# A convolution, attention and expert-mixture kernel on one core: the kv sum's constant part moved to PE, and three more slots for the last images' gate broadcasts

## The chip, the core and the metric

The kernel runs on one core of a Trainium2 chip. Its engines are TensorE (PE, matmuls; its weight loads are listed as PEld), VectorE (DVE), ScalarE (ACT), GpSimd (POOL) and SyncE (SP, which here only issues transfers); 16 DMA engines move data between the chip's memory (DRAM, HBM) and the core's on-chip memory. PE's results go to a memory of their own, PSUM, from which DVE and ACT read them. Each engine has its own program, built in a fixed order, in which an instruction waits until the semaphores that it names have come.

The metric is the time of one execution in microseconds of device time. Before the change five runs were made; the median counts. A profile is one more execution, recorded by the hardware.

## What is computed

The input `x` is 32 images of 128 channels by 56 by 56 pixels (3136 tokens of 128 numbers each, in float32). Cut to what matters here:

```python
x = x + conv3x3(sign(group_norm(x)), sign(w)) * Alpha       # layer 0
t = to_tokens(x)                                            # layer 1, by image: 3136 x 128
u = layer_norm(t)
q, k, v = u @ Wq + bq, u @ Wk + bk, u @ Wv + bv
kv = sum(k * v, axis=tokens)                                # one number for each channel
t = t + q * kv
u = layer_norm(t)
p = softmax(u @ router_w + router_b);  best two of 8 experts, their weights made to add to 1
t = t + sum of the two weights times (u @ expert_w[e] + expert_b[e])
```

The sum over tokens never needs k and v themselves. The layer norm's mean is taken out by centring the weights, so u is the tokens times the reciprocal deviation. With G = uᵀu (128 by 128, "gram"), s = the sum of u over the tokens (a column), n = 3136 and all vectors by output channel c,

`kv[c] = sum over d of Wk[d,c] * ((G Wv)[d,c] + bv[c]*s[d]) + bk[c] * (sᵀ Wv)[c] + n*bk[c]*bv[c]`

The change is about how this line is computed, and about the last step of the expert mixture.

## The kernel before

**Planner.** The kernel describes its work as some thousands of small steps with `at(due, key, engine, work, do, after, take, free, delay)`. `due` is when the step should come, `work` its length in microseconds as its author put it down, `after` the steps it needs, `take` and `free` the slots of a ring of buffers that it takes and frees. Before anything is emitted, `in_order` lays all steps out in time by these numbers, and the instructions are emitted in that order. So the order on each engine is fixed when the program is built. If a `work`, a ring or a dependency changes anywhere, the order of later steps can change on all engines.

**Images.** Images are worked on some 60 us apart by their due times, and two or three overlap: convolution of image i+1 (nine matmuls for each of seven stripes, `cv`), transposes to tokens (`xt`), statistics, `gram` of image i, the kv steps, projection `q` with the matrix `move`, routing on DVE, gates, experts. The x and token buffers are three each (`x_all`, `tok_all`, image i uses number i mod 3). Images 0 to 27 form four groups. Their first 8 or 12 token chunks take all eight experts ("dense"); the other tokens are sorted by pair of experts, sent to DRAM with indirect transfers, worked on in tiles (`turn`, `to`), and fetched back (`back`, then `back_ps`, copied to `o` and stored). Images 28 to 31 are in no group and all their 25 chunks are dense, so the kernel's end is dense work of images 30 and 31 with the fetching back of the last group laid between.

**The kv steps of one image.** They follow the gram matmuls and share one PSUM slot, ring `acc`, of size one. `gram_out` (L754, ACT) copies G and the column s to `g_sb`. `kv_1` (L758, PE) makes `gv` = G Wv. `kv_2` is three DVE operations: `prod` = bv*s + gv (L763), times Wk (L765), plus `wv_bk`*s (L767), where `wv_bk` = Wv*bk was made once. `kv_3` (L772, PE) sums `prod` over its 128 rows with a matmul by `ones`, which gives kv as a row repeated on all partitions. `kv_4` (DVE) adds the constant `n_bkbv` (L777), then makes the left part of `move` (L779) and `bq_kv` (L781). `kv_5` (L786, PE) turns kv into a column with a one-column matmul. `kv_6` (L792, L794, DVE) multiplies the router's weights by that column, and again by bq. `kv_7` (L801, L802, PE) makes two small products of it, `kv_8` (L806, L808, ACT) copies them into `move` and `cq`. Then `project` (L863) can start. `bias` (L815) adds `bq_kv` to the tokens on DVE.

**Set-up.** `prepare` runs once, after the first image's convolution: PE centres the weights (`centred`, L377 and L379), DVE makes `move`'s right part, `wv_bk` (L394), `n_bkbv` (L395), `masks` (L402) and, from the expert biases, `eb_sum` and `eb_w` (L407 to L415). All of DVE's set-up stands in DVE's order in the order in which the code issues it.

**Dense experts.** For a block b of four chunks (512 tokens) there are four units k = 0 to 3, each two experts. The gates of an image are transposed on PE (`gate_turn`, L1017), copied by ACT, and stored by SP to DRAM (`gate_store` L1038, `parts_store` L1061). `spread` (SP) loads from there: for k = 0 first `gt` (L1129, three transfers), then for every unit `bc` (L1132), the gates of two experts, 512 tokens each, repeated over 128 partitions, 512 KB. `bc` is a ring of four slots. `gated` (L1141, DVE) multiplies it with the tokens `tt`, which frees the slot; `experts` (L1153 and L1159, PE) does `eb_w` once in a block and two matmuls for each unit, 512 columns each; `finish` (L1170, DVE) and `store` (L1175, SP) end the block. SP issues everything in one order: loads of x, gates, broadcasts, result stores (L1175, and L1471 for the fetched-back blocks). A store that waits for its data holds everything behind it.

Of the kernel before, what the change touches and what calls it, by code (L numbers as in the profile page):

```python
# [54 lines left out]
C = 128  # L55
# [34 lines left out]

P = 60.0
# [8 lines left out]
    t_in=3, turned=2, v=3, w=2, back=12, sent=4, o=2,  # L100
# [85 lines left out]
def conv_attn_moe_kernel(  # L186
# [173 lines left out]
    wv_bk = const.tile([C, C], F32, name="wv_bk")  # L360
    n_bkbv = const.tile([C, C], F32, name="n_bkbv")
# [5 lines left out]
    def prepare():  # L367
# [25 lines left out]

        nc.vector.tensor_mul(wv_bk, wv_sb, bk_bc)  # L394
        nc.vector.scalar_tensor_tensor(  # L395
            n_bkbv, bk_bc, float(n_tok), bv_bc, ALU.mult, ALU.mult
        )

# [145 lines left out]
    def plan_image(i: int):  # L544
# [215 lines left out]
        def kv_2():  # L760
            tok_sum = d["g_sb"][:, C : C + 1]
            prod = spool.tile([C, C], F32, tag="prod", bufs=1, name=f"prod_{i}")
            nc.vector.scalar_tensor_tensor(prod, bv_bc, tok_sum, d["gv"], ALU.mult, ALU.add)  # L763
            yield
            nc.vector.tensor_mul(prod, prod, wk_sb)  # L765
            yield
            nc.vector.scalar_tensor_tensor(prod, wv_bk, tok_sum, prod, ALU.mult, ALU.add)  # L767
            d["prod"] = prod

        def kv_3():  # L770
            d["kv_ps"] = ps_acc.tile([C, C], F32, tag="acc", name=f"kv_ps_{i}")
            nc.tensor.matmul(d["kv_ps"], lhsT=ones, rhs=d["prod"], start=True, stop=True)  # L772

        def kv_4():

            kv = spool.tile([C, C], F32, tag="prod", bufs=1, name=f"kv_{i}")
            nc.vector.tensor_add(kv, n_bkbv, d["kv_ps"])  # L777
# [4 lines left out]
            d["kv"] = kv  # L782

        def kv_5():
            d["kvc"] = ps_acc.tile([C, 1], F32, tag="acc", name=f"kvc_ps_{i}")
            nc.tensor.matmul(d["kvc"], lhsT=d["kv"], rhs=ident[:, :1], start=True, stop=True)  # L786

        def kv_6():
# [3 lines left out]
            nc.vector.scalar_tensor_tensor(kr[:, 0, :], rw_sb, d["kvc"], one, ALU.mult, ALU.mult)  # L792
# [24 lines left out]
        for g in range(n_blk):  # L817
# [18 lines left out]
        for j, (engine, work, do) in enumerate(kv_steps, 1):  # L836
# [1041 lines left out]
```

## Time and profile before

| | us |
|---|---|
| median of 5 runs | 2284.51 |
| lowest and highest run | 2275.41, 2289.13 |
| profiled execution | 2265.75 |
| its span, first to last instruction | 2264.1 |
| PE idle in the span | 160 |
| PE idle from 100 to 500 | 33 |
| PE idle from 500 to 2040 | 78 |
| PE idle from 2100 to the end | 22 |

The profiled execution is 18.8 us shorter than the median of the timed runs, so a sum made from its rows belongs to 2265.75 and not to 2284.51. The granted TensorE clock was 0.975 of full on average. An engine's busy time doesn't hold the issuing of transfers, and the ends of matmuls are modelled; one float32 matmul shows as two records, each with its own weight load.

The memory traffic of the end is heavy: in the last fortieth of the span 291 GB/s were moved, against a mean of 198 over the whole.

### The profile page before, as it was taken

Reading aid. Unit: us, or ns where it says so; the run is one execution under the profiler, and the core shown is the slowest. Engines: PE = TensorE matmul, PEld = TensorE weight load, DVE = VectorE, ACT = ScalarE, POOL = GpSimd, SP = SyncE. Lnnn points to the kernel's source line nnn. Section 1 sums busy time; section 2 is a strip of 40 time slices with the busy share of each in tenths; the row PEclk is TensorE's granted clock in tenths of the full one; section 3 lists DMA queues with packets and bytes.
Section 4 is the critical chain, followed back from the end, with each engine's and each line's share of the span. In section 5 each row is a group of like instructions: output and inputs, shape, how many; then the busy total and the mean of one; then the engine's idle time right before and its main releaser. Section 6 shows DMA issues by size and latency. Waiting matters only on the chain.

```text
span 2264.1 us, 45320 instructions
## 1 busy us (share of the span) xinstructions
PE 2103.9 (93%) x12074; PEld 1449.0 (64%) x12074; DVE 1971.0 (87%) x6074; ACT 1527.6 (67%) x4917; POOL 1037.2 (46%) x1013
## 2 busy tenths in 40 slices
PE   5899999899999999989999999988999999999889
PEld 2666556556777776557776776655677666675544
DVE  4899999999999999878898889988888897789765
ACT  5667776667888887658777876655868776574311
POOL 3044443333333235656443544666654546234563
PEclk9999999999999999989999999999999999999899
DMA  4155544455655555567677766667768777878688
GB/s 167 30 168 167 171 155 151 139 176 188 193 163 152 184 175 170 170 203 252 175 218 232 228 194 202 215 202 244 231 177 250 210 211 244 257 217 267 209 278 291
DMA packets 324364, 448.58 MB, mean 198 GB/s; under 512 B 61832, under 2 KB 222128, under 8 KB 324112
## 3 DMA queue, kind: packets, MB, share of 16 engines
q1 hardware_dynamic: 294384, 382.80, 53.9%
q0 software_dynamic: 28144, 56.14, 8.1%
q10 hardware_dynamic: 1584, 6.75, 0.8%
q8 instruction: 102, 1.67, 0.3%
q14 instruction: 150, 1.23, 0.2%
HBM read 319.51 MB, written 126.00 MB: 197 GB/s over the span
## 4 chain that ended last, share of the span: by engine, by line
PE 42%; DVE 7%; issue 3%; ACT 3%; DMA 2%; SPq 1%; another core or an unknown queue 1%; POOL 0%; DVEq 0%; ACTq 0%; POOLq 0%
PE ff L1159 15%; PE cv L642 6%; PE to L1687 6%; PE gram L744 3%; PE q L863 3%; DVE gated L1141 2%; PE back_ps L1459 2%; PE xt L667 1%; PE turn L1669 1%; PE l L1114 1%; ACT v L1705 1%; DMA t_in<-rows 1%; DMA bc<-gp 1%; ACT w L1712 1%
## 5 line engine op out<-in xcount | busy, mean ns | idle before, releaser
L1365 POOL DMA_INDIRECT rows<-tok,row_no x428 | 510.6, 1193 | 580.7 <-ACT tok L1358 284.3
L1159 PE MATMUL ff<-gated,ew_d 128*128 128x512 f32 (+1 forms) x1536 | 708.6, 590 | 24.1 <-DVE gated L1141 15.6
L1444 POOL DMA_INDIRECT back<-res,res_no x428 | 495.3, 1157 | 446.0 <-PE back_ps L1459 249.3
L1141 DVE TENSOR_TENSOR gated<-tt,bc 128x1024 f32<-128x1024 f32 x384 | 449.9, 1178 | 75.0 <-PE ff L1159 31.4
L642 PE MATMUL cv<-xs,w_bin 128*128 128x440 bf16 (+3 forms) x2016 | 428.8, 361 | 19.0 <-ACT xs L599 10.9
L1159 PEld LDWEIGHTS ff<-gated,ew_d 128*128 128x128 f32 x1536 | 273.3, 192 | 259.6 <-issue 209.7
L1705 ACT ACTIVATE v<-to,t_in 128x128 f32<-128x128 f32 x528 | 255.1, 484 | 135.2 <-PE to L1687 68.2
L642 PEld LDWEIGHTS <-w_bin 128*128 128x128 bf16 x2016 | 199.2, 100 | 186.7 <-issue 37.8
L1687 PEld LDWEIGHTS to<-ew_s,turned 128*128 128x128 f32 x2112 | 261.2, 194 | 57.1 <-issue 30.2
L877 ACT ACTIVATE qs<-q,r 128x136 f32<-128x136 f32 (+1 forms) x800 | 248.3, 411 | 64.4 <-PE q L863 38.2
L1687 PE MATMUL to<-ew_s,turned 128*128 x2112 | 274.0, 279 | 16.9 <-ACT turned L1675 8.7
L735 ACT ACTIVATE y<-tok,r 128x128 f32<-128x128 f32 (+1 forms) x800 | 256.4, 426 | 26.2 <-remote 12.7
L863 PE MATMUL q<-move,x 128*128 128x144 f32 (+1 forms) x1600 | 242.8, 297 | 16.1 <-ACT move L806 5.6
L863 PEld LDWEIGHTS q<-move,x 128*128 128x128 f32 (+1 forms) x1600 | 215.7, 194 | 47.1 <-issue 19.2
L744 PEld LDWEIGHTS gram<-y 128*128 128x128 f32 (+1 forms) x1600 | 201.7, 192 | 47.5 <-issue 36.4
L744 PE MATMUL gram<-y 128*128 128x129 f32 (+1 forms) x1600 | 217.2, 280 | 6.3 <-issue 5.8
L682 DVE BATCH_NORM_STATS2 st<-tok 128x6 f32<-128x128 f32 (+1 forms) x800 | 184.8, 277 | 33.0 <-ACT tok L673 24.2
L1712 ACT ACTIVATE w<-to,t_in 128x128 f32<-128x128 f32 x528 | 208.8, 395 | 0.0
L893 DVE BATCH_NORM_STATS2 st<-tok 128x6 f32<-128x128 f32 (+1 forms) x800 | 198.0, 284 | 6.2
L673 ACT COPY tok<-xt 128x512 f32<-128x512 f32 (+1 forms) x224 | 121.6, 564 | 94.7 <-PE xt L667 65.9
L890 DVE TENSOR_TENSOR tok<-tok,qs 128x408 f32<-128x408 f32 (+1 forms) x288 | 155.8, 541 | 29.2 <-ACT tok L882 23.0
L653 DVE SCALAR_TENSOR_TENSOR x<-cv,alpha_col,x 128x448 f32<-128x448 f32 x224 | 150.8, 674 | 33.9 <-PE cv L642 10.2
(229 smaller groups left out, 2894.6 us busy)
## 6 DMA issues: line engine op xcount, KB each, us to landing
bc<-gp SPq DMA_DIRECT2D x368, 512.0 KB
x<-in_x_dram SPq DMA_DIRECT2D x116, 392.0 KB
t_in<-rows SPq DMA_DIRECT2D x528, 66.0 KB
res<-v SPq DMA_DIRECT2D x132, 256.0 KB
out_dram<-o SPq DMA_DIRECT2D x100, 256.0 KB
out_dram<-tt SPq DMA_DIRECT2D x92, 256.0 KB
rows<-zeros SPq DMA_DIRECT2D x116, 66.0 KB
rows<-tok,row_no POOLq DMA_INDIRECT x428
```

The lines of the kernel that those rows point to most:

```text
L642: nc.tensor.matmul(cv[:, r0:r1, c0:c1], lhsT=w_bin[:, t, :], rhs=xs[:, b * ROWS + dy + r0 : b * ROWS + dy + r1, dx + c0 : dx + c1], start= ...
L735: nc.scalar.mul(y[:n, j, :C], d["tok"][:n, c, :C], d["r1"][:n, c : c + 1])
L744: nc.tensor.matmul(d["gram"], lhsT=y[:n, j, :C], rhs=y[:n, j, :], start=(c == 0), stop=(c == n_ck - 1),)
L863: nc.tensor.matmul(p[:n, k, :], lhsT=d["x"][:, c * C : c * C + n], rhs=move, start=True, stop=True,)
L877: nc.scalar.mul(qs[:n, k, :], p[:n, k, : C + N_EXP], d["r1"][:n, c : c + 1])
L1141: nc.vector.tensor_tensor(g[:, :, :n], d["tt", b][:, :n].unsqueeze(1).to_broadcast([C, 2, n]), d.pop(("bc", b, k))[:, :, :n], ALU.mult,)
L1159: nc.tensor.matmul(d["ff", b][:, :n], lhsT=ew_d[:, e * C : (e + 1) * C], rhs=g[:, j, :n], start=False, stop=(e == N_EXP - 1),)
L1365: dma = nc.gpsimd.indirect_dma_start(out=groups[group]["rows"], out_offset=bass.IndirectOffsetOnAxis(ap=d["row_no"][:n, c - n_dense : c - ...
L1444: dma = nc.gpsimd.indirect_dma_start(out=d["back", c][:n, :], out_offset=None, in_=groups[group]["res"][: quads_of(group) * WIDE, :], in_o ...
L1687: nc.tensor.matmul(p[:, k, j, :], lhsT=t[:, n * C : (n + 1) * C], rhs=ew_s[:, bass.ds(d["cols", q][j][n], C)], start=True, stop=True,)
L1705: nc.scalar.activation(d["v", q][:, n, :], p[:, k, 0, :], AF.Identity, bias=row[:, C + 2 : C + 3], scale=row[:, C : C + 1],)
L1712: nc.scalar.mul(d["w", q][:, n, :], p[:, k, 1, :], row[:, C + 1 : C + 2])
```

## The change

It has two parts, and the second has no data in common with the first.

**The kv sum.** The term with bv is merged into the constant matrix: `wv_bk` becomes Wv*bk + Wk*bv, made in the set-up. `kv_2` is one DVE operation, `prod` = Wk * gv. `kv_3` makes four matmuls into one PSUM tile of 129 columns: s repeated as stationary operand (a read with step 0) times `wv_bk`, plus `ones` times `prod`, give the row on all partitions; `prod` times a column of `ones`, plus `wv_bk` times s, give the same sums as a column. `kv_5` is gone. `kv_6` reads the column from that tile and adds the constant `rw_n`, the router's weights times n*bk*bv as a column, for which the set-up has one more matmul (`n_col_ps`) and one more DVE operation. `kv_6` and `kv_4` both follow `kv_3`. In the planner `kv_3` counts 0.70 in place of 0.25, `kv_2` 0.21 in place of three pieces.

**Three more slots.** From image 30 on every second unit's broadcast (of seven units the 2nd, 4th and 6th) goes to a third of the x buffer of image 29, which nothing reads after that image's projection. This is a ring `late` of three beside `bc` of four. The transfer itself has the same size and the same queue.

```diff
+LATE, LATE_IN = 30, 29
...
+        wk_bv = spool.tile([C, C], F32, tag="prod", bufs=1, name="wk_bv")
+        nc.vector.tensor_mul(wk_bv, wk_sb, bv_bc)
         nc.vector.tensor_mul(wv_bk, wv_sb, bk_bc)
+        nc.vector.tensor_add(wv_bk, wv_bk, wk_bv)
         nc.vector.scalar_tensor_tensor(
             n_bkbv, bk_bc, float(n_tok), bv_bc, ALU.mult, ALU.mult
         )
+        p = ps.tile([C, 1], F32, tag="ps", name="n_col_ps")
+        nc.tensor.matmul(p, lhsT=n_bkbv, rhs=ident[:, :1], start=True, stop=True)
+        nc.vector.tensor_scalar(rw_n, rw_sb, p, None, ALU.mult)
...
+    n_late = n_tok // (2 * WIDE)
+
+    def late_of(i, n):
+
+        turn = n % (2 * n_late + 1)
+        return turn // 2 if i >= LATE and turn % 2 else None
...
         def kv_2():
-            tok_sum = d["g_sb"][:, C : C + 1]
-            prod = spool.tile([C, C], F32, tag="prod", bufs=1, name=f"prod_{i}")
-            nc.vector.scalar_tensor_tensor(prod, bv_bc, tok_sum, d["gv"], ALU.mult, ALU.add)
-            yield
-            nc.vector.tensor_mul(prod, prod, wk_sb)
-            yield
-            nc.vector.scalar_tensor_tensor(prod, wv_bk, tok_sum, prod, ALU.mult, ALU.add)
-            d["prod"] = prod
+            d["prod"] = spool.tile([C, C], F32, tag="prod", bufs=1, name=f"prod_{i}")
+            nc.vector.tensor_mul(d["prod"], wk_sb, d["gv"])
 
         def kv_3():
-            d["kv_ps"] = ps_acc.tile([C, C], F32, tag="acc", name=f"kv_ps_{i}")
-            nc.tensor.matmul(d["kv_ps"], lhsT=ones, rhs=d["prod"], start=True, stop=True)
+            p = ps_acc.tile([C, C + 1], F32, tag="acc", name=f"kv_ps_{i}")
+            tok_sum = d["g_sb"][:, C : C + 1]
+            nc.tensor.matmul(
+                p[:, :C], lhsT=tok_sum.to_broadcast([C, C]), rhs=wv_bk, start=True, stop=False
+            )
+            nc.tensor.matmul(p[:, :C], lhsT=ones, rhs=d["prod"], start=False, stop=True)
+            nc.tensor.matmul(p[:, C:], lhsT=d["prod"], rhs=ones[:, :1], start=True, stop=False)
+            nc.tensor.matmul(p[:, C:], lhsT=wv_bk, rhs=tok_sum, start=False, stop=True)
+            d["kv_ps"] = p
...
-        def kv_5():
-            d["kvc"] = ps_acc.tile([C, 1], F32, tag="acc", name=f"kvc_ps_{i}")
-            nc.tensor.matmul(d["kvc"], lhsT=d["kv"], rhs=ident[:, :1], start=True, stop=True)
...
-            nc.vector.scalar_tensor_tensor(kr[:, 0, :], rw_sb, d["kvc"], one, ALU.mult, ALU.mult)
+            nc.vector.scalar_tensor_tensor(
+                kr[:, 0, :], rw_sb, d["kv_ps"][:, C:], rw_n, ALU.mult, ALU.add
+            )
...
-            ("PE", 0.25, kv_1), ("DVE", [0.26, 0.21, 0.27], kv_2), ("PE", 0.25, kv_3), ("DVE", [0.19, 0.41], kv_4),
-            ("PE", 0.25, kv_5), ("DVE", [0.14, 0.14], kv_6), ("PE", 0.46, kv_7), ("ACT", 0.15, kv_8),
...
+            (1, "PE", 0.25, kv_1, ["gram_out"], ["acc"], []),
+            (2, "DVE", 0.21, kv_2, ["kv_1"], [], [("acc", ("kv_1", i))]),
+            (3, "PE", 0.70, kv_3, ["kv_2"], ["acc"], []),
+            (4, "DVE", [0.19, 0.41], kv_4, ["kv_3"], [], [("acc", ("kv_3", i))]),
+            (6, "DVE", [0.14, 0.14], kv_6, ["kv_3"], [], [("acc", ("kv_3", i))]),
+            (7, "PE", 0.46, kv_7, ["kv_6"], ["acc"], []),
+            (8, "ACT", 0.15, kv_8, ["kv_7", "kv_4"], [], [("acc", ("kv_7", i))]),
...
-            bc = bpool.tile([C, 2, WIDE], F32, tag="bc", bufs=4, name=f"bc_{i}_{b}_{k}")
+            slot = late_of(i, b * N_EXP // 2 + k)
+            if slot is None:
+                bc = bpool.tile([C, 2, WIDE], F32, tag="bc", bufs=4, name=f"bc_{i}_{b}_{k}")
+            else:
+                bc = x_all[LATE_IN % HELD][:, slot * 2 * WIDE : (slot + 1) * 2 * WIDE]
+                bc = bc.rearrange("c (j t) -> c j t", j=2)
...
+                bc_ring = "bc" if late_of(i, n) is None else "late"
...
+                    + (
+                        [("project", LATE_IN, j) for j in range(len(q_groups))]
+                        if bc_ring == "late"
+                        else []
+                    ),
+                    take=[bc_ring] if k else [bc_ring, "gt"], delay=SPREAD_LANDS,
```

More of the change, by code (lines that the diff above doesn't have):

```diff
@@ L832, in plan_image @@
         kv_steps = (
-            ("PE", 0.25, kv_1), ("DVE", [0.26, 0.21, 0.27], kv_2), ("PE", 0.25, kv_3), ("DVE", [0.19, 0.41], kv_4),
-            ("PE", 0.25, kv_5), ("DVE", [0.14, 0.14], kv_6), ("PE", 0.46, kv_7), ("ACT", 0.15, kv_8),
-        )
-        for j, (engine, work, do) in enumerate(kv_steps, 1):
-            after = [(f"kv_{j - 1}", i) if j > 1 else ("gram_out", i)]
+            (1, "PE", 0.25, kv_1, ["gram_out"], ["acc"], []),
[5 more added lines that the diff above has]
+            (8, "ACT", 0.15, kv_8, ["kv_7", "kv_4"], [], [("acc", ("kv_7", i))]),
+        )
+        for j, engine, work, do, after, take, free in kv_steps:
+            after = [(k, i) for k in after]
             if j == 4:
@@ L841, in plan_image @@
                 after += [("route_1", i - 2), ("project", i - 2, 8)]
-            at(
-                s + 75 + j, (f"kv_{j}", i), engine, work, do, after=after,
-                take=["acc"] if engine == "PE" else [],
-                free=[] if engine == "PE" else [("acc", (f"kv_{j - 1}", i))],
-            )
+            at(s + 75 + j, (f"kv_{j}", i), engine, work, do, after=after, take=take, free=free)
         for g in range(n_blk):
@@ L1206, in plan_image @@
                     + [("gated", i, n - 1) if n else ("gated", i - 1, last_unit)],
-                    take=["gated"], free=[("bc", ("spread", i, n))], slack=0.5,
+                    take=["gated"], free=[(bc_ring, ("spread", i, n))], slack=0.5,
                 )
```

11 lines of the change are left out of this document (5 added, 6 removed).

## The prediction

> **What bounds the kernel now.** I read the busy shares first, then busy time by stretch, then the groups of the kv steps, then the timeline at the three places where the change moves something: the set-up, the last image's kv chain, the last image's gates.
>
> ```profile
> PE 2103.9 (93%) x12074; PEld 1449.0 (64%) x12074; DVE 1971.0 (87%) x6074; ACT 1527.6 (67%) x4917; POOL 1037.2 (46%) x1013
> ```
>
> By the whole span PE is the bound, with DVE behind it. By stretch (columns: stretch, length, busy PE, PEld, DVE, ACT, POOL, granted clock, DMA share, GB/s) it is not one story:
>
> ```profile
> 100.00:500.00 400.00, 367.05 (x2063) 240.52 (x2061) 387.90 (x1371) 272.64 (x917) 168.95 (x160) 0.97 0.47 152
> 500.00:2040.00 1540.00, 1462.00 (x8810) 1045.88 (x8810) 1354.53 (x4127) 1133.86 (x3644) 739.31 (x628) 0.98 0.67 206
> 2100.00:2126.00 26.00, 19.15 (x102) 13.26 (x100) 18.61 (x48) 5.36 (x15) 13.88 (x13) 0.86 0.51 165
> 2136.00:2184.00 48.00, 44.31 (x143) 21.13 (x144) 43.23 (x95) 9.69 (x28) 32.29 (x27) 1.00 0.92 301
> 2184.00:2214.00 30.00, 21.88 (x68) 11.40 (x69) 12.61 (x22) 3.48 (x10) 19.25 (x19) 0.72 0.78 244
> 2214.00:2264.00 50.00, 46.86 (x152) 23.32 (x151) 29.54 (x32) 6.73 (x14) 15.20 (x13) 0.98 0.81 287
> ```
>
> From 100 to 500 DVE sets the pace (97%, while PE has 33 us free); from 500 to 2040 PE does (95%); at 2100 to 2126 and 2184 to 2214 neither does, and the clock drops: two stalls of the last image.
>
> The kv steps in the groups (busy us, mean ns of one | idle of the engine before them and what ended it; one f32 matmul is two records):
>
> ```profile
> L767 DVE SCALAR_TENSOR_TENSOR prod<-wv_bk,g_sb,prod 128x128 f32<-128x128 f32 x32 | 11.0, 344 | 1.0 <-DVE st L682 0.6
> L763 DVE SCALAR_TENSOR_TENSOR prod<-bv_bc,g_sb,gv 128x128 f32<-128x128 f32 x32 | 10.9, 342 | 10.6 <-PE gv L758 7.6 <-PE gt_ps L1017 2.8
> L772 PE MATMUL kv_ps<-prod,ones 128*128 128x128 f32 x64 | 13.9, 297 | 4.8 <-DVE prod L767 3.5 <-issue 1.3
> L786 PE MATMUL kvc_ps<-ident,kv 128*128 128x1 f32 x64 | 10.2, 229 | 7.0 <-issue 3.7 <-DVE kv L777 3.3
> ```
>
> **Part 1, set-up: +2.4.** Program order of the changed kernel: n_col_ps is PE's last set-up matmul, and DVE's rw_n, which reads it, stands ahead of masks, eb_sum, eb_w, a conv_add (L653) and the total of image 2 (L588).
>
> ```profile
> 43.17 0.28 DVE L395 SCALAR_TENSOR_TENSOR n_bkbv<-bk_bc,bv_bc 128x128 f32<-128x128 f32 x1
> 45.91 0.22 DVE L415 CAST eb_w<-eb_sum 72x128 bf16<-72x128 f32 x1
> 48.47 0.60 PE L667 MATMUL xt<-ident,x 128*128 128x128 f32 x4
> 49.22 0.16 DVE L596 TENSOR_SCALAR neg_gm<-gm_ps 128x1 f32<-128x1 f32 x1 [2.04 <-PE gm_ps L592]
> ```
>
> Now DVE goes straight on. Then it stands from 43.9 (0.56 later, for two more 128x128 operations) until PE's set-up ends at 48.5 plus 0.14 for n_col_ps, so about 49.1; behind it 2.7 us (43.4 to 46.1) to eb_w, 0.4 of statistics and 0.6 of conv_add, giving 52.8. PE's xt needs that conv_add: 52.9 instead of 48.5, and behind it the group mean, the signs, and image 1's convolution. +4.4. Some comes back at once: between gv and the first q of image 0 PE's order holds 6 us of other work instead of 12 (13.1 us went by, 67.90 to 81.02), so q of image 0 starts earlier; from 0 to -5, I take -2 because the displaced convolutions still have to run.
>
> **Part 2, DVE: -5.6 where DVE sets the pace.** Two of three prod operations go: 342 + 344 = 0.69 us, with their gaps 0.70. The column's kr stays one operation. Eight chains lie in 100 to 500: -5.6. The added matmuls there (8 x 0.36, next part) lie in PE's 33 us of idle time; without that cover they cost 2.9. Elsewhere DVE's gain (22 x 0.70 from 500 to 2040) is off the path, where DVE is 88% busy.
>
> **Part 3, PE: +4 where PE sets the pace.** kv_3 grows from one 128x128 matmul to two plus two of one column; kv_5's column matmul goes. Net one 128x128 and one 128x1. In a full queue a gram matmul takes 0.22 (eight records in 0.89), and kvc_ps 0.14 (2040.20 to the next start at 2040.34): +0.36 per image, 22 chains from 500 to 2040, +7.9. The lowest bound is 0 (all of it in idle time), the highest the unhidden records, 2 x 0.297 + 2 x 0.229 = 1.05 each, +23. I take the queue's pitch, as these matmuls stand in a full queue. No row has a stationary operand read with step 0, as tok_sum is now; its nearest is an ordinary load, 0.19, hidden under matmuls. Against it stand waits that ended at kv_ps, kvc_ps, kr_ps or the first q: 9.4 us from 500 to 2040 in PE's waits. The chain loses two DVE operations, one trip PE-DVE-PE and DVE work queued ahead of kr, but the planner also gives it less cover; I take -4 of 0 to -9.
>
> **Part 4, last kv chain: -4.** Nothing is left to cover it:
>
> ```profile
> 2117.35 0.49 PE L772 MATMUL kv_ps<-prod,ones 128*128 128x128 f32 x2 [0.32 <-issue]
> 2121.49 0.58 PE L786 MATMUL kvc_ps<-ident,kv 128*128 128x1 f32 x2 [3.66 <-issue]
> 2124.16 0.60 PE L801 MATMUL kr_ps<-kr,wq_t 128*128 128x8 f32 x2 [2.08 <-DVE kr L792]
> 2126.38 6.13 PE L863 MATMUL q<-move,x 128*128 128x144 f32 x24 [0.89 <-ACT move L806]
> ```
>
> From gv's end (2116.2) to q is 10.2 us, 3.6 of them DVE waits before finish and kv that no row explains (2.45, 1.19). The new chain: prod 0.29, four matmuls about 1.1, kv 0.29, kr 0.22, move 0.29, bq_kv 0.28, kr 0.22, kr_ps 1.1, move 0.17, some 0.4 for hops: 4.4. So -2.2 if the unexplained waits stay, -5.8 if they go. Then 24 q records took 6.13 at a granted clock of 0.50, and 3.21 for image 30 at 1.00: up to -2.9 more. I take -4 of 0 to -8.7.
> The Trainium skill ("TensorE: Matmul & The Clock Gate", Part 1, What's actually happening) says that the array falls to half clock after an idle window of about 3.4 us and needs a busy one to come back; the gap of 3.66 and the 6.13 agree. By that rule alone gaps of at most 2 us would keep the clock, and this part would be -2.9 from the clock by itself.
>
> **Part 5, last gates and the three slots: -11.** In the old order PE's transpose of image 31's gates (2183.18) has 11.0 us of work between it and image 31's first experts, in the new one 18.8: a block of image 30 (eight expert matmuls at 0.86, eb_w, transposes) now lies behind it. DVE makes the gates before unit 3_3 rather than after 4_0, so PE doesn't wait for them.
>
> ```profile
> 2195.42 0.69 SPq L1132 DMA_DIRECT2D bc<-gp  x1
> 2201.26 0.36 SPq L1471 DMA_DIRECT2D out_dram<-o  x1
> 2201.67 1.39 SPq L1132 DMA_DIRECT2D bc<-gp  x3
> 2202.08 3.78 PE L1159 MATMUL ff<-gated,ew_d 128*128 128x512 f32 x4 [2.19 <-DVE gated L1141]
> 2209.14 3.78 PE L1159 MATMUL ff<-gated,ew_d 128*128 128x512 f32 x4 [3.28 <-DVE gated L1141]
> ```
>
> SP issued one broadcast, then stood 5 us at a result store that waited for PE, so the next three left at 2201.67 and PE ran at half clock. From 2183.18 to 2214.42 PE did 15.5 us of work at full pitch: 15.7 lost. Afterwards the same path (gate transpose to first unit on PE, 18.9) is covered by 18.8, the store ahead of the second broadcast belongs to a transpose further up PE's queue, and the third to seventh broadcast no longer wait for a fourth slot. Left over: about 1.5, and 3 for transfers that come at once: -11. Bounds: 0 to -15.7. The slots by themselves are worth little: of DVE's waits for bc from 2040 on (7.1) 5.8 is the one above. Seven transfers under way instead of four also means that SP meets its own limit, as each issue waits for the eighth before it (from 2040 on 3.5 us of waits at L1132 ended so).
> The Trainium skill ("DMA: Bandwidth & Descriptors", Specifications) gives about 358 GB/s of HBM per core, which speaks against more slots. The trace shows 6 us stretches at up to 397, so the trace decides; by the rule the 38 MB moved from 2126 on (10 x 198 + 48 x 301 + 30 x 244 + 50 x 287 kB) would need an estimated 106 us of the 138 they had, and this part could still be had.
>
> **Sum**, on the profiled execution (2265.75 us, span 2264.1): 2.4 - 5.6 + 4 - 4 - 11 = -14.2. It was 19 us faster than the median of the runs, 2284.51, so I take the difference over: 2270.
>
> **Rivals.**
> A, the tail is held by transfers: from 2214 to 2250 the DMA share is 0.91 to 1.04 in most 6 us stretches. Earlier gates would then only fill the hole before (share 0.65, 0.49 from 2190 to 2202, some 5 us) and part 5 shrinks to -3. Sum -6, 2278. For it: the shares. Against: the holes at 2106 to 2124 and 2130 to 2136 (0.27) count as well.
> B, slower: PE waits for DVE in every chain. The new order puts only 1.7 us of PE work between gv and kv_3 for images 3 to 8 where 3.4 to 5.7 stood, and PE is in order: all queued behind stands too. Thirty chains (all but the first and last); from 0.85 us each the sum passes +11.4; at 1.0 it is +16, 2300. For it: in 100 to 500 kv_ps waited three times, 3.1 us. Against: PE's waits at these lines average under 0.6 per chain now, and DVE has one prod operation instead of three to do there.
> C, the chip's order settles as before and only parts 1 to 3 count, with the rest lost: +1, 2285.
>
> **How the numbers follow.** A change under 0.5% (11.4 us) can't be told from none. Forecast 0.48, A 0.20, C 0.14, B 0.18. The forecast's own range is 2252 to 2273; with A, C and part of B the range is 2252 to 2295. Faster 0.48, same 0.34, slower 0.18.
>
> **What would show it.** DVE's rw_n waits about 5 us near 44. Busy DVE falls by some 22 us, busy PE rises by 10 to 15. The 8 chains from 100 take 5 us less. The gap from gv to q of image 31 is under 7 us and its q runs near 3.2 per 24 records. Image 31's first two expert units follow without gaps over 3 us. Wrong if PE idles at kv_ps or kr_ps grow past 25 us, or if the stall after the last gates is still over 8 us.

## The result and the profile after

The changed kernel took 2284.64 us (median of 44 runs, 2260.62 to 2312.53), the kernel before 2280.81 us (86 runs beside them and earlier, 2259.95 to 2310.37). The ratio is 1.001, 95% interval 0.9994 to 1.0025: some +2.3 us, between -1.4 and +5.7. That is no change that can be told, and the forecast of -14.2 lies outside the interval.

The profiled execution after took 2297.86 us (span 2295.9), 32 us more than the one before. Runs of one kernel differ by some 10 us here; only six of the 86 runs before were faster than the profile before, and only four of the 44 after slower than the profile after. So I don't read this difference, and go by stages and by several executions. First the busy shares after:

```profile
PE 2118.3 (92%) x12204; PEld 1465.5 (64%) x12204; DVE 1953.0 (85%) x6013; ACT 1532.0 (67%) x4917; POOL 1041.5 (45%) x1013
```

DVE has 18.0 us less work (forecast 22), PE 14.4 more (forecast 10 to 15): the change does what it says. The 14.4 belong to this pair of profiles; in the three pairs of the experiments whose two kernels ran side by side DVE has 17 to 20 us less and PE 5 to 12 more. By stretch, and the groups of the kv steps, with the columns of before:

```profile
100.00:500.00 400.00, 369.15 (x2099) 244.43 (x2097) 382.12 (x1361) 277.29 (x925) 168.67 (x160) 0.98 0.46 148
500.00:2040.00 1540.00, 1445.36 (x8703) 1035.98 (x8704) 1322.52 (x4038) 1114.83 (x3578) 735.24 (x616) 0.97 0.67 204
```

```profile
L784 PE MATMUL kv_ps<-wv_bk,g_sb 128*128 128x128 f32 x64 | 13.4, 292 | 3.0 <-DVE prod L779 1.9 <-issue 0.9
L787 PE MATMUL kv_ps<-prod,ones 128*128 128x128 f32 x64 | 12.6, 280 | 0.0
L789 PE MATMUL kv_ps<-g_sb,wv_bk 128*128 128x1 f32 x64 | 11.9, 253 | 0.5 <-issue 0.5
```

PE stands 3.0 us ahead of kv_ps in all 32 chains together, 4.8 before; with kr_ps it is 12.3 us, 8.4 of them in one chain. Rival B, in which PE waits for DVE in each chain, did not come. The set-up, timeline of DVE and then of PE:

```profile
47.71 0.29 DVE L399 TENSOR_TENSOR wk_bv<-wk_sb,bv_bc 128x128 f32<-128x128 f32 x1 [4.30 <-PE centred L381]
49.27 0.24 DVE L407 TENSOR_SCALAR rw_n<-rw_sb,n_col_ps 128x8 f32<-128x8 f32 x1 [0.54 <-PE n_col_ps L406]
...
52.51 0.66 DVE L670 SCALAR_TENSOR_TENSOR x<-cv,alpha_col,x 128x448 f32<-128x448 f32 x1
```

```profile
48.66 0.33 PE L393 MATMUL wq_t_ps<-ident,wq_sb 128*128 128x128 f32 x1
48.88 0.35 PE L406 MATMUL n_col_ps<-ident,n_bkbv 128*128 128x1 f32 x2
...
53.22 1.11 PE L684 MATMUL xt<-ident,x 128*128 128x128 f32 x4 [3.11 <-DVE x L670]
```

DVE does stand for 4.3 us and PE's xt comes at 53.2, as forecast to 0.3 us. But the wait that shows is not that of rw_n (0.54). It stands a few instructions earlier, at wk_bv. This new tile has the tag "prod" with one buffer, centre lies in it, and PE's centred matmuls read centre until 47.7. PE itself came to n_col_ps only at 48.88, behind the rest of its set-up, so without the wait at wk_bv rw_n would have stood almost as long: there are two waits, one behind the other, and the forecast saw the second.

The last image's kv chain, PE, DVE and GpSimd:

```profile
2149.26 0.44 PE L775 MATMUL gv<-wv_sb,g_sb 128*128 128x128 f32 x2
...
2151.70 0.36 PE L789 MATMUL kv_ps<-g_sb,wv_bk 128*128 128x1 f32 x2
2160.49 0.60 PE L816 MATMUL kr_ps<-kr,wq_t 128*128 128x8 f32 x2 [8.44 <-DVE kr L805]
```

```profile
2154.25 0.22 DVE L1191 TENSOR_TENSOR tt<-tt,ff 128x64 f32<-128x64 f32 x1 [3.30 <-remote]
2160.01 0.29 DVE L795 TENSOR_TENSOR kv<-n_bkbv,kv_ps 128x128 f32<-128x128 f32 x1 [5.54 <-remote]
```

```profile
2147.06 0.95 POOL L1471 DMA_INDIRECT back<-res,res_no  x1 [8.59 <-PE back_ps L1486]
2148.32 0.95 POOL L1471 DMA_INDIRECT back<-res,res_no  x1 [0.30 <-issue]
...
2157.09 0.95 POOL L1471 DMA_INDIRECT back<-res,res_no  x1 [0.30 <-issue]
```

All matmuls of kv_ps had ended by 2152.06 in the record, DVE had nothing else to do, and yet kv began at 2160.01. "remote" means that the sign (the semaphore that tells DVE that PE is done) came, but no instruction had ended shortly before it: PE's semaphore rose at 2159.99, some 8 us late. All that time GpSimd issued gathers of result rows, nine in a row, 1.26 us apart, the last ending at 2158.04. From the start of gv to the start of q it was 10.6 us before, and is 12.6 now. The two waits that no row explained before (2.45 and 1.19, the second ahead of the same kv) are of this kind.

The last gates (PE, then SP's queue, then DVE's products):

```profile
2210.52 0.60 PE L1033 MATMUL gt_ps<-ident,gate 128*128 128x128 f32 x4
...
2231.34 0.66 PE L1180 MATMUL ff<-gated,ew_d 128*128 128x64 f32 x4 [1.22 <-DVE gated L1162]
...
2235.44 3.69 PE L1180 MATMUL ff<-gated,ew_d 128*128 128x512 f32 x4 [2.82 <-DVE gated L1162]
...
2247.82 2.50 PE L1180 MATMUL ff<-gated,ew_d 128*128 128x512 f32 x4 [2.09 <-issue]
```

```profile
2219.16 0.37 SPq L1054 DMA_DIRECT2D gp<-gt_sb  x1
...
2221.02 3.38 SPq L1077 DMA_DIRECT2D gb<-gt_parts  x7
...
2227.68 0.35 SPq L1153 DMA_DIRECT2D bc<-gp  x1
```

```profile
2234.16 1.23 DVE L1162 TENSOR_TENSOR gated<-tt,bc 128x1024 f32<-128x1024 f32 x1 [1.90 <-DMA bc<-gp]
2236.58 1.29 DVE L1162 TENSOR_TENSOR gated<-tt,x 128x1024 f32<-128x1024 f32 x1 [1.20 <-DMA x<-gp]
...
2246.53 1.23 DVE L1162 TENSOR_TENSOR gated<-tt,bc 128x1024 f32<-128x1024 f32 x1 [3.99 <-ACT tt L1137]
```

The path from the gates' transpose to image 31's first unit on PE took 18.9 us before, and the prediction carried that number over. It takes 24.9 now (2210.52 to 2235.44): the gates' first store left SP 8.6 us after the transposes' start where it had been 4.6, the first broadcast 17.2 after it where it had been 12.2. So the PE work put behind the transposes (20.9 us of the 24.9) does not cover it, and PE stands for 6.1 us again where it had stood for 8.0. DVE's first products of image 31 waited for the landing of their broadcasts (1.90 and 1.20); the product behind PE's third wait waited for a copy on ACT.

### The profile page after: what moved, and what is told of

It reads as the page before. It is cut to its first block, busy times and chain, and to the rows that moved or that the text cites. A ratio compares the mean times of both kernels' runs of the same rounds, so it can differ in the third digit from the quotient of the medians.

```text
span 2295.9 us, 45560 instructions
## 1 busy us (share of the span) xinstructions
PE 2118.3 (92%) x12204; PEld 1465.5 (64%) x12204; DVE 1953.0 (85%) x6013; ACT 1532.0 (67%) x4917; POOL 1041.5 (45%) x1013
## 3 DMA queue, kind: packets, MB, share of 16 engines
q14 instruction: 149, 1.22, 0.2%
## 4 chain that ended last, share of the span: by engine, by line
PE 59%; DVE 8%; another core or an unknown queue 3%; DMA 3%; issue 2%; ACT 2%; SPq 1%; DVEq 0%; ACTq 0%
PE ff L1180 19%; PE cv L659 10%; PE to L1714 9%; PE q L879 5%; PE gram L761 5%; PE turn L1696 2%; PE xt L684 2%; DVE gated L1162 2%; DMA bc<-gp 2%; PE back_ps L1486 2%; PE l L1130 1%; DVE st L909 1%; PE ff L1174 1%; DVE tok L906 1%
## 5 line engine op out<-in xcount | busy, mean ns | idle before, releaser
L1392 POOL DMA_INDIRECT rows<-tok,row_no x428 | 530.7, 1240 | 610.1 <-ACT tok L1385 334.7
L1471 POOL DMA_INDIRECT back<-res,res_no x428 | 481.1, 1124 | 464.2 <-PE back_ps L1486 271.7
L1162 DVE TENSOR_TENSOR gated<-tt,bc 128x1024 f32<-128x1024 f32 (+1 forms) x360 | 424.7, 1186 | 71.5 <-PE ff L1180 26.7
L659 PEld LDWEIGHTS <-w_bin 128*128 128x128 bf16 x2016 | 199.9, 100 | 184.6 <-issue 37.4
L879 PE MATMUL q<-move,x 128*128 128x144 f32 (+1 forms) x1600 | 245.0, 296 | 11.8 <-ACT tok L898 3.3
```

The source lines that it names most:

```text
L659: nc.tensor.matmul(cv[:, r0:r1, c0:c1], lhsT=w_bin[:, t, :], rhs=xs[:, b * ROWS + dy + r0 : b * ROWS + dy + r1, dx + c0 : dx + c1], start= ...
L879: nc.tensor.matmul(p[:n, k, :], lhsT=d["x"][:, c * C : c * C + n], rhs=move, start=True, stop=True,)
L1162: nc.vector.tensor_tensor(g[:, :, :n], d["tt", b][:, :n].unsqueeze(1).to_broadcast([C, 2, n]), d.pop(("bc", b, k))[:, :, :n], ALU.mult,)
L1392: dma = nc.gpsimd.indirect_dma_start(out=groups[group]["rows"], out_offset=bass.IndirectOffsetOnAxis(ap=d["row_no"][:n, c - n_dense : c - ...
L1471: dma = nc.gpsimd.indirect_dma_start(out=d["back", c][:n, :], out_offset=None, in_=groups[group]["res"][: quads_of(group) * WIDE, :], in_o ...
```

## The experiments

Eighteen experiments were run in six sets; the kernels of one set share a chip and the runs of the kernel before. The kernel before itself fell into two kinds: 2172 us in two sets, 2253 to 2266 in four, which is nearer the 2281 of the result. Both kinds came from the chip with number 4, so it is no fixed property of that number.

What is found in one kind and not in the other is the late sign. I counted the waits of DVE and ACT over 0.5 us on PE's semaphore alone in which the semaphore rose over 1 us after the last recorded end of a signalling matmul. Before: 33, late by 66 us in all; after: 35 (102 us, some overlapping). In the four sets of 2253 us and more there are 27 to 42 wherever gathers and issue density were left alone; in the two sets of 2172 us there is none. ACT's signs were never late, DVE's three times in all 20 profiles, by 1.1 to 1.2 us. I call the sets "late" and "on time". The changed kernel as it is was run only in late sets.

**Parts alone, on time.** The new sum without the slots returns None for every slot:

```
-        return turn // 2 if i >= LATE and turn % 2 else None
+        return None
```

> The changed kernel without the three slots: the new sum of keys times values alone (every broadcast in the four old buffers). Its order on PE keeps the earlier transpose of image 31's gates (ahead of block 30_4's transposes). Theory S (the sum of the prediction holds, and something outside the change eats it): kv parts 2.4-5.6+4-4 = -3, and the last gates -8 of the -11, as only the fourth slot's wait comes back: about -11 against the kernel before, stage by stage, though not in the total. Theory B (PE waits for DVE in each chain): +8 to +16. Theory Z (the new chain is worth nothing and costs nothing): 0 +- 3.

2166.46 against 2172.34 us, ratio 0.9976 (0.9963 to 0.9989): -5.2. The slots alone are the hunks on late_of, bc and bc_ring, put into the kernel before:

> The kernel before with only the three slots in the dead image buffer. Here the gates' transpose of image 31 has about 10 us of PE work behind it up to image 31's first unit, much as before (11.0). Theory S: the gain of part 5 hangs on the earlier gates and not on the slots, so 0 to -3. Theory that the slots are the gain: -8 to -11. Rival A (transfers hold the tail): 0, and the tail's DMA share as high as before. A loss of 3 or more would mean that more transfers at once delay the stores.

2169.71 us, 0.999 (0.998 to 0.9999): -2. The new sum is worth something on time, under half of what theory S gave it; the planner's new order, with its earlier transposes of the last gates, is in this number too. The last chain on time, kv only:

```profile
2022.99 0.44 PE L775 MATMUL gv<-wv_sb,g_sb 128*128 128x128 f32 x2
...
2024.50 0.36 PE L789 MATMUL kv_ps<-g_sb,wv_bk 128*128 128x1 f32 x2
2025.38 0.39 PE L816 MATMUL kr_ps<-kr,wq_t 128*128 128x8 f32 x2 [0.52 <-DVE kr L805]
```

gv to q is 3.6 us here and 6.4 with the old sum (slots only): -2.9, where the forecast had given -2.2 to the chain by itself.

**Gathers as plain transfers, on time.** In both kernels the gathers fetch consecutive rows of the same size, not the rows that belong to the tokens:

```
-            dma = nc.gpsimd.indirect_dma_start(
-                out=d["back", c][:n, :],
...
+            lo = (c - n_dense) * C
+            dma = nc.gpsimd.dma_start(
+                d["back", c][:n, :], groups[group]["res"][lo : lo + n, :]
+            )
```

> The changed kernel with the 428 gathers of result rows issued as plain transfers of consecutive rows of the same size (the sorted images' output is then that of other rows). Theory G (the stops in which PE, DVE and ACT stand together for 3 to 12 us come from GpSimd's back-to-back indirect transfers): few stops over 2 us are left in the profile (10 over 1.5 us, 37.9 us in all, in the changed kernel's profile), the time falls by 10 to 30 us, the scatter of the runs from some 10 us to under 5. Against the kernel before with the same edit: -10 to -14 by the prediction's sum. Theory N (the stops are from elsewhere): as many stops, time within 5 us of the changed kernel, the same scatter.

> The kernel before with the same edit of the 428 gathers. Theory G: few stops over 2 us, 10 to 25 us under the kernel before, scatter under 5 us; its difference to the changed kernel with the edit is then the change's own effect. Theory N: within 5 us of the kernel before, the same scatter.

2157.48 (changed) and 2159.25 us (before), 0.993 and 0.9945 of the kernel before. There were no late signs to lose in this set, so the 13 to 15 us are another cost of the gathers, and theory G was not tested yet. The pair differs by 1.8 us, not by 10 to 14.

**The two kernels again, late.** The next set fell on the other kind.

> The changed kernel as it is. Of the two profiles shown with the result, both from a chip on which the kernel before takes 2281 us, each holds some 30 waits of DVE and ACT that PE's semaphore ended 1 to 11 us after the matmul's recorded end (63 and 99 us in all); in the first four experiments, on a chip where the kernel before takes 2172 us, there is not one. Theory L (the late signs of PE belong to the chip, and they hide and eat the change's gain): on a chip without them the changed kernel is 7 to 14 us faster than the kernel before (kv alone gave -5.2 and the slots -2), beyond the interval. Theory Z (the change is worth nothing anywhere): within 3 us of the kernel before on either chip. Theory S (the sum of the prediction): -14 on a chip without late signs.

> The kernel before as it is, for a profile beside that of the changed kernel on the same chip. All theories: the same time as the kernel before, within 1 us. Theory L: on a chip without late signs no wait above 1 us behind a recorded end of PE, and the last image's stalls are smaller than in the profile shown: gv to q of image 31 7 us or less instead of 10.6, and after the last gates under 6 us of idle PE, so that parts 4 and 5 had less to win than the 15 us forecast. Theory S: the same two stalls as in the profile shown.

The changed kernel 2257.87, the kernel before 2265.77 (0.9971, 0.9939 to 1.0003); but the copy of the kernel before had 2260.37 and the same ratio against its own other runs. Twelve runs of a late set tell no difference under 0.3%. Their profiles count: gv to q of image 31 is 11.8 us in the changed order (kr_ps waits 8.4), 9.8 in the old one.

**The set-up.** First the column's matmul alone was moved to image 0's chain:

> The changed kernel with the constant column's matmul taken out of the set-up: it joins image 0's column matmuls, and rw_n is made in image 0's chain; the order on every engine is otherwise the same. By part 1 of the prediction DVE no longer waits near 44 us, gv of image 0 starts 4.4 us earlier; the gain at the end is 4.4 if all later stages only shift, 2.4 if 2 us had come back at once, and 0 if DVE's backlog in 100 to 500 takes it up.

2262.4 us; wk_bv still waited 4.30, gv of image 0 started 0.6 us earlier, which is less than executions of one kernel differ there. So the named wait was not the one that held the set-up. Then the buffer was changed too, so that both waits are gone:

```
-        wk_bv = spool.tile([C, C], F32, tag="prod", bufs=1, name="wk_bv")
-        nc.vector.tensor_mul(wk_bv, wk_sb, bv_bc)
+        nc.vector.tensor_mul(n_bkbv, wk_sb, bv_bc)
...
-        nc.vector.tensor_add(wv_bk, wv_bk, wk_bv)
+        nc.vector.tensor_add(wv_bk, wv_bk, n_bkbv)
```

> The previous try took rw_n's matmul out of the set-up and gv of image 0 came only 0.6 us earlier, since DVE's 4.3 us wait stands before wk_bv: this new tile shares the one buffer of centre, which PE's centred matmuls read until 47.5. Here the product goes to n_bkbv's tile first, and rw_n is made in image 0's chain. Theory P (the pool buffer is the wait): no DVE wait over 1 us between 43 and 49, gv of image 0 near 78 as in the kernel before (82 in the changed one); the end is 2 to 4 us earlier than the changed kernel's if later stages keep it, 0 if DVE's backlog takes it up. Prediction's part 1 (rw_n's wait for PE is the loss): was wrong already by e7, and would give nothing here either.

> The changed kernel with the set-up mended (as e9), a second time. Where PE's signs are not late (the kernel before takes some 2172 us): the new sum alone gave -5.2, the slots alone -2, the mended set-up 2 to 4 more, so 7 to 11 us under the kernel before if the three add up, with an interval clear of 1. By the pair with plain gathers (-1.8 with the set-up unmended): 4 to 6 under. Where they are late (2250 to 2285): 0.993 to 1 again.

2255.27 (0.9968, 0.9936 to 1.0000) and 2259.78 us (0.9983, 0.9954 to 1.0011). gv of image 0 starts at 68.8 and 67.0 us of the span, 70.1 to 73.4 in five executions with the set-up as changed, 67.4 and 67.9 before. The DVE wait is gone (here from the kernel of e17, which has this set-up):

```profile
42.87 0.24 DVE L396 COPY move<-rw_sb 128x8 f32<-128x8 f32 x2 [1.28 <-ACT rw_sb L384]
43.02 0.29 DVE L398 TENSOR_TENSOR n_bkbv<-wk_sb,bv_bc 128x128 f32<-128x128 f32 x1
```

The buffer alone, with rw_n's matmul left in the set-up, was not run. Both sets were late, so each interval reaches 1, and what the mended set-up is worth on time was not measured to the end.

**Price of PE's work.** `for _ in range(5):` before the matmul of gv.

> The changed kernel with four more copies of the matmul gv in each image (each overwrites the same tile, the output is the same): by the pitch of a full queue 4 x 0.22 = 0.9 us more of PE per image, and as much more latency in the chain. Where PE sets the pace this costs 0.9 per image, where DVE does it costs 0: +20 (22 images from 500 to 2040) if the prediction's picture of the stages holds, +28 if PE sets the pace everywhere, under +8 if PE's idle time takes the added matmuls up. On a chip with late signs of PE: nearer +28, as PE is then behind everywhere.

2281.31 us, 1.0064 (1.0036 to 1.0093); against the changed kernel of the same set +0.9%, some 21 of 28 us. Most of any PE work is paid, which rules out that PE's idle time takes it up; whether it is paid everywhere or only from 500 to 2040 can't be told.

**Price of DVE's work.** Four `nc.vector.tensor_mul(kv, wq_sb, kv)` behind bq_kv.

> The changed kernel with four more 128x128 products on DVE per image behind bq_kv, off the chain (they overwrite kv, which nobody reads any more). At 0.28 each with their gaps that is about 0.9 to 1.1 us of DVE per image. If DVE sets the pace from 100 to 460: gv of image 0 to gv of image 8 grows from 382 by 7 to 9 us, and little elsewhere, so 8 to 15 in all. If it doesn't: under 3 there. The same slope upward as the change should have had downward.

gv of image 0 to gv of image 8 took 389.1 us, 6.9 over the mean of 382.2: DVE sets the pace there for three quarters of 8 x 1.12. But the total missed: 2286.17 us, 1.0162 (1.0109 to 1.0214), +25 to +48 us, the whole 32 x 1.12 = 36 or nearly. So added DVE work is paid for beyond 500 too, where the prediction had called it off the path. Part of that comes by the chain, for the products do not lie off it: they stand ahead of the second kr, and in 16 of the 32 images ahead of both.

```profile
2141.41 1.27 DVE L801 TENSOR_TENSOR kv<-wq_sb,kv 128x128 f32<-128x128 f32 x4
2142.60 0.22 DVE L811 SCALAR_TENSOR_TENSOR kr<-kr,bq_col,ones 128x8 f32<-128x8 f32 x1
```

Without image 31 PE stands 14.4 us at kr_ps here and 0.2 to 2.3 in the other late executions of the changed order. So 36 us is an upper bound for DVE's pace alone.

**What holds the tail.** Half the bytes (one expert's gates are sent and used for both of a unit, the other's are left out), and the last gates' stores from another queue:

```
+            m = 1 if i >= LATE else 2
             nc.sync.dma_start(
-                bc[:, :, :n],
-                d["gp"][b, 2 * k : 2 * k + 2, :n].unsqueeze(0).to_broadcast([C, 2, n]),
+                bc[:, :m, :n],
+                d["gp"][b, 2 * k : 2 * k + m, :n].unsqueeze(0).to_broadcast([C, m, n]),
```

> The changed kernel with the gate broadcasts of images 30 and 31 cut to half their bytes (one expert of each pair is sent and used for both, so the gates of the other are left out). Order and issues are the same. From gv of image 31 to the end the changed kernel takes 144 to 147 us on chips with late signs. Rival A (transfers hold the tail): 10 us or more less there, as about 14 of 39 MB go. Theory Q (the path of the last gates through SP's queue holds it, 24 us from the gates' transpose to the first unit where 18.9 was forecast): 1 to 4 us less, and the idle time ahead of image 31's first two units stays 4 us or more. If the waits ahead of DVE's products go but the end stays: PE's own work is the bound there.

```
-            nc.sync.dma_start(
+            ring = nc.scalar if i == LATE + 1 else nc.sync
+            ring.dma_start(
```

> The changed kernel with image 31's eight stores of gates issued from ScalarE's queue, so they don't stand behind broadcasts and result stores in SP's (the first left 7.1 us after the transposes' end, the seven others took SP 3.5 us). Theory Q: first unit of image 31 some 16 to 19 us after the gates' transpose instead of 24, PE's 5.5 us of idle time there go, gv of image 31 to end 3 to 6 us shorter. Rival A: the broadcasts land as late as before, under 1 us. If ScalarE stands at the stores: its copies for the next blocks come later, and nothing is won.

> The changed kernel as it is, as the reference of the other three on this chip. On a chip with late signs of PE: within 0.3% of the kernel before, some 8 us of idle PE ahead of kr_ps of image 31 again, as in all four executions of this order so far (8.4, 8.4, 7.1, 8.3). On a chip without them: 0.5 us there, and 5 to 8 us faster than the kernel before.

2246.3, 2261.77 and 2260.46 us (0.9939, 0.9989, 0.9985). From gv of image 31 to the end: 137.3, 144.4 and 144.9. Half the bytes give 7.6 us there, the free queue 0.5; the other late executions of the changed order lie between 143.9 and 146.6, so only the first stands clear of scatter. Of the three waits behind the gates (1.22, 2.82 and 2.09 in the profile after) half the bytes leave one:

```profile
2186.35 0.38 PE L1175 MATMUL ff<-gt,eb_w 72*128 72x512 bf16 x1
2187.96 1.98 PE L1181 MATMUL ff<-gated,ew_d 128*128 128x512 f32 x4 [1.23 <-DVE gated L1163]
```

Theory Q falls: with the stores on ScalarE's queue the first one left 1.2 us after the transposes' start instead of 9.0, but image 31's first unit still came 24.6 us after that start (24.2 with them in SP's queue), and PE's stalls only came earlier (2.9 us at 70.3 after gv instead of 3.0 at 82.3; 5.7 us in all against 6.1). With half the bytes the same path takes 21.4 us. Rival A is right in kind, if a little under its 10 us: most of the tail's waits go when the broadcasts' transfers get shorter.

**What makes the signs late.** The plain gathers again, now in a late set, and GpSimd with two transfers under way (`IN_FLIGHT = 2`):

> The changed kernel with its 428 gathers as plain transfers once more (the sorted images' output is that of other rows), meant for a chip with late signs. Theory G (GpSimd's series of indirect gathers delay PE's signs): the stop ahead of kr_ps of image 31 falls from 7 to 8.5 us to under 1, the late signs from 30 to 40 to under 15 (the scatters stay indirect), the time is 20 us or more below the changed kernel's. Theory N (the chip stops PE by itself, power or clock): kr_ps of image 31 still waits 7 us or more, as many late signs, under 10 us gained. On a chip without late signs nothing is told here beyond the third experiment.

> The kernel before with the same edit, beside the last on the same chip. The difference of the two is the change's own effect without the gathers' series: on the chip without late signs it was -2 us (2157.5 against 2159.3). Theory G: the same here, 0 to -4. The prediction's sum would be -14. By the same theory gv to q of image 31 takes 6 to 7 us here and 3 to 4 in the changed kernel.

> The changed kernel with two of GpSimd's indirect transfers under way instead of four, so that it waits for a landing before each issue but two. Theory G in the form that it is the density of issues: fewer and shorter stops, kr_ps of image 31 waits less than 4 us, 5 to 20 us faster than the changed kernel on a chip with late signs. If only the length of the series counts: series as long or longer, the stop stays 7 us or more, and the later gathers cost 0 to 10 us.

With plain gathers 2181.96 (changed) and 2181.16 us (before) against 2253.29 in the same set, ratios 0.9704 (0.9658 to 0.975) and 0.9699: 71 and 72 us, and runs within 6 and 9 us of each other instead of 38. Late signs: 9 and 7, none over 1.7 us (the scatters were still indirect). The pair itself differs by +0.8 us. It is still 22 to 24 us slower than the same pair on time, so the gathers are not all that divides the two kinds of sets. kr_ps of image 31 in the changed kernel:

```profile
2044.07 0.36 PE L789 MATMUL kv_ps<-g_sb,wv_bk 128*128 128x1 f32 x2
2044.96 0.39 PE L816 MATMUL kr_ps<-kr,wq_t 128*128 128x8 f32 x2 [0.52 <-DVE kr L805]
```

The same instructions, 0.52 instead of 8.44. With two under way there was no late sign either, with every gather still indirect; but the gathers came too late:

```profile
PE back_ps L1486 <- DMA back<-res,res_no: 168.2, 62, 13.0
```

(engine's waits: us in all, times, longest), and the kernel took 2423.18 us (1.0775). So it is the indirect transfers issued back to back that go with PE's late signs, in a late set: taking away either the indirect gathers or their density takes them away. Whether GpSimd's issuing or the transfers of scattered rows do it, no run tells apart. In all ten late executions of the changed order with gathers and density as they were kr_ps of image 31 waits 7.1 to 8.4 us (in e8, with its longer gv, 3.5 and 4.8 in two places), and DVE's kv begins 0.4 to 2.0 us after the last issue of the series of nine, whatever stood ahead of it. In the old order the chain's signs came 1 to 3 us late each inside the same series; it ended 9.8 us after gv, and q began at 9.8 and 10.6. In a set on time the same series stands there and nothing is late; what puts a set in one kind or the other was not found.

Last, a density in between, with the mended set-up (`IN_FLIGHT = 3`):

> The changed kernel with the set-up mended as in e9 and three indirect transfers under way instead of four. Theory G by density: the late signs fall to between none (two under way) and 30 to 40 (four), and PE waits for gathers between 168 us (two) and under 15 (four). If the pitch of a series only has to pass the landing time by a little, the late signs go and the gathers still come in time: 30 us or more below the kernel before. If both effects are in proportion: as fast as the kernel before or up to 60 us slower.

It fell on a set on time: 2209.74 against 2172.55 us (1.0178, 1.0161 to 1.0196), PE waiting 37.4 us for gathers. So it is slower where there is nothing to mend; whether it wins in a late set wasn't tried. It shows one thing more, in one execution each: gv of images 0 to 17 starts 3.3 to 5.3 us of the span earlier than with kv only on time (66.6 against 71.6 for image 0, 4.0 for image 17), so what the set-up wins is kept until the gathers come in.

## Why the prediction failed

Each stage against its part. The late columns take the two profiles of the kernel before and those of the changed order (five executions with the set-up as changed for part 1, eight that differ in set-up or tail alone for parts 2 to 4, seven for part 5; standard error up to 0.6 us, 5 for part 3, of the changed side alone: the two profiles before differ by up to 3.6). The last column is the pair with plain gathers, on time.

| part, stage | forecast | late: before, changed | measured late | on time, plain |
|---|---|---|---|---|
| 1: start to gv of image 0 | +2.4 | 67.7, 71.6 | +3.9 | +5.7 |
| 2: gv 0 to gv 8 | -5.6 | 385.1, 382.2 | -2.8 | -2.7 |
| 3: gv 8 to gv 31 | +4 | 1660.9, 1665.3 | +4.4 | -1.3 |
| 4: gv 31 to its q | -4 | 10.2, 12.2 | +2.0 | -3.1 |
| 5: q of 31 to the end | -11 | 137.9, 132.7 | -5.2 | -0.3 |
| sum | -14.2 | | +2.3 | -1.7 |

That the late column adds up to the measured +2.3 is chance, with an error of 5 in one of its rows. The late pair with plain gathers, one execution each, gives +4.1, -3.2, +5.5, -2.9 and +1.5. The clock's 2.9 us of part 4 lies in the last stage here, so parts 4 and 5 are best read together: -15 forecast, -3.2 late, -3.4 and -1.4 with plain gathers. This is the term that failed.

- **Part 5** failed at the sentence "Afterwards the same path (gate transpose to first unit on PE, 18.9) is covered by 18.8". The path's length is not its own: moved forward it took 24.9, and it did not get shorter when its stores left SP's queue early (24.6), only with half the bytes (21.4). The step counted a path and its cover, and put the broadcasts' transfers at nothing; they end PE's waits wherever the gates stand. I had the shares of 0.91 to 1.04 in rival A and gave them 0.20. Half the bytes give 7.6 us, the queue 0.5. Rival A's price for the part, -3, lies between what came (-5.2 late, -0.3 and +1.5 with plain gathers).
- **Part 4** was right in the chain where signs are on time (-2.9 and -3.1) and wrong in the runs it was made for. The step that failed is "-5.8 if they go": the unexplained waits of 2.45 and 1.19 were the mark of the late signs, and the shorter chain did not take them away. In both orders q began only when GpSimd's series of nine had ended (at 9.8 and 10.6 with 9.8 for the series; at 11.1 to 12.6 with 8.8), so the shorter chain seems only to have reached the wait sooner. The clock's term failed too: the first 24 records of q took 5.80 us at 0.54 in the profile after, and 4.87 at 0.65 on time without the slots, where PE's longest gap between gv and q was 0.52 us; gaps under 2 us did not keep the clock.
- **Part 2** was mis-sized: 0.56 us of busy time came off DVE per chain, not 0.70 (18.0 over 32: the rows of prod fall by 22.1, from 31.0 to 8.9, but the records of neighbouring operations overlap), DVE sets the pace for three quarters by e16, and the added PE work costs a quarter by e8's stage (384.0 against 382.2 for 7.2 us, one execution against a scatter of 1.4). Estimated from these, 8 x 0.56 x 0.77 less 8 x 0.36 x 0.25 is -2.7.
- **Part 3** can't be judged: +4.4 with an error of 5 in late sets is its size, -1.3 on time is not. Its working left out that DVE's work is paid for in this stage too. By the prices of e16 and e8 as they stand, taking 18 us off DVE for 5 to 14 more on PE should even have won some 7 us or more; part 1 takes 4 of that back, and the rest stays open.
- **Part 1**: the size of the stall was right (4.4 forecast, 3.9 measured late), but with some luck: a wait for a buffer, not in the forecast, stood ahead of the one it named and ended 1.6 us before it. The -2 that was to come back at once did not come.
- **Rivals.** A was right for the tail. B did not come: 3.0 us at kv_ps and 8.4 of kr_ps in one chain, not 0.85 in thirty. C, the change's net near zero (+1), is nearest to the result, but by parts 4 and 5 lost to other work, not by an order that settled back. Neither of the two signs that were to show the forecast wrong came (12.3 of 25 us at kv_ps and kr_ps, 6.1 of 8 us after the last gates), though it was wrong.

The Trainium skill ("Perfetto Trace Analysis", Tensor Engine Instruction) says that a matmul's recorded end is an estimate and that PE's semaphore is pushed only once PSUM has acknowledged the last bytes. The sign 7.9 us after the recorded end of kv_ps agrees with such an order of events, and leaves it open whether the matmul, its write or the sign was held up; no run here tells these apart.

## What to carry to other kernels

A gap between two instructions is only worth closing by a shorter chain if what ends it lies in the chain: look at the time at which the sign came, not at the operation it is booked on, and treat "remote" and waits that no row explains as a cost of something else that runs at that time. When a step is moved forward, its path has to be counted again in its new surroundings, queue by queue, and not carried over. And a tile that takes a single-buffered tag waits for everybody who reads the tag's last tile: look for that, and then for the next wait behind it.

## What the runs showed that was not expected

- With back-to-back indirect transfers of GpSimd, four under way, PE's signs come up to 10.8 us late in some sets of runs and never late in others; plain gathers took 71 and 72 us off the two kernels there, many times what the change was about.
- The kernel before differs by 80 to 110 us between sets (2172 and 2253 to 2281 us).
- Two transfers under way instead of four cost 170 us, though GpSimd is busy only 45% of the time in the profile after: PE waited 168 us for gathers to land.
- No version was shown to beat both kernels. The new sum without the slots beat the kernel before on time (0.9976, 0.9963 to 0.9989); the mended set-up had the lower median in both its late sets, with intervals that reach 1.
